# Last level of a graph layer's edge sums as two half levels, with bucket counts kept in SBUF

## The chip, the cores and the metric

One core of a Trainium2 chip runs the kernel. The metric is the device time of one execution in microseconds; a kernel's figure is the median over its runs. The engines are named as the profile names them: PE (TensorE matmul, with PEld for its weight loads), DVE (VectorE), ACT (ScalarE), POOL (GpSimd) and SP (SyncE, which here only issues DMAs).

## What is computed

A graph layer over 12500 nodes of 64 features and 212500 edges that come sorted by `dst`, in float32:

```python
h = jnp.maximum(_layernorm(x, axis=-1), 0.0)
edge_in = jnp.concatenate([h[row], h[col], dist], axis=1)      # row = src, col = dst
e = jax.nn.silu(edge_in @ eW1 + eb1)                           # 129 -> 128
e = jax.nn.silu(e @ eW2 + eb2)                                 # 128 -> 128
agg = jax.ops.segment_sum(e, row, num_segments=h.shape[0])
node_in = jnp.concatenate([h, agg], axis=1)
out = x + jax.nn.silu(node_in @ nW1 + nb1) @ nW2 + nb2
```

## The kernel before

The nodes are cut into NB = 100 **buckets** of L = 125 (node n lies in bucket n mod 100), four buckets make a **quad** (25 quads). `eW1` is split: `ta` and `tb` hold, per node, the parts of the first product that belong to `src` and to `dst`, so an edge needs `ta[src] + tb[dst] + dist * w + b`.

**Sending.** Edges come in `dst` order, in 208 **blocks** of 1024. For a block, `send` (line 406) picks the `tb` rows by a one-hot matmul on a window of neighbouring nodes (`qp`, L418: eight matmuls, float32), ACT copies the result to SBUF tiles `qs` (L429), adds the place of the source node (L435), and POOL scatters it by eight indirect DMAs (L442, 128 rows each) into `q` in DRAM: one slot per edge, ordered by source bucket and by **rank**, the number of the edge within its bucket. `count` (line 338) finds the ranks of the next block: DVE marks each edge's bucket in `oh` (L348) and sums it into `each` (L356); two matmuls (`before`, L382, and, a block later, `rest`, L341) add it to `full`, a PSUM tile that accumulates over all blocks; DVE multiplies `oh` by `full` into `mine` (L396), reduces it to `rank` (L398) and writes the scatter's addresses `to` (L400, four buffers). `pick` (L378) is the one-hot list that `send` needs. `count` and `send` are generators; `send_all` (line 463) steps them in turn, three **pieces** a block, count first.

**Summing.** A bucket's 2304 ranks are split into 12 **levels** (LEVELS, line 54: tiles of 128 ranks per bucket, the block after which they are full, spare ranks that are zeroed beforehand). Batches are (level, quad); a **step** handles four tiles of 128 edges. `fetch` (line 484) loads a quad's ranks `qt` and its `ta` rows `a` through SP, NQ = 4 batches ahead. Per step: `lr` (L518) and `oneT` (L523) turn node numbers into a one-hot; `pt` (L532, L538) transposes the rows and adds `a` by that one-hot; SiLU on ACT (L542); `p2` (L570, with the bias from L564); SiLU (L574); `seg` (L584) sums edges into nodes with the one-hot `one` (L551), in one PSUM bank; `s_add` (L595) adds the sum to `aggT`. In the last level each quad's `nodes` (line 235) then makes the output: `z` (L242, L245), SiLU `zs` (L247), `o` (L251), `os` (L254), and two DMAs.

**Order.** PE, DVE, ACT and SP run in the order written out by hand. `turn` (line 602) lists a step's parts with the number of steps that each is ahead, and four hooks (None). At hooks the loop (line 880) emits send pieces so that level w's blocks, with a lead of three, are sent when its first fetch is due (`marks`), then two pieces of the feed (layer norm, tables), then one stage of a quad's `nodes`. PSUM has `mm` (four tiles, shared by `lr`, `pt`, `qp`, `z`, `o`), `p2` (two), `full` and `seg` (one each).

If a count breaks a level's limits, a flag sends the whole sum through a slow general path.

Of the kernel before, what the change touches and what calls it, by code (L numbers as in the profile page):

```python
# [49 lines left out]
G = 4  # L50
# [4 lines left out]
LEVELS += [(1, 184, 0), (1, 194, 32), (1, 202, 96), (1, 208, 128)]  # L55
ENDS = [P * sum(n for n, _, _ in LEVELS[: w + 1]) for w in range(len(LEVELS))]
# [15 lines left out]
def tile_gnn(ctx: ExitStack, tc: tile.TileContext, x, src, dst, ew, eW1, eb1, eW2, eb2, nW1, nb1, nW2, nb2, out):  # L72
# [105 lines left out]
    rest = const.tile([P, P], BF16, name="rest")  # L178
    nc.vector.tensor_scalar(rest, ahead_i, 0.5, float(G), op0=OP.is_lt, op1=OP.mult)
# [79 lines left out]
    NQ = 4  # L259
# [5 lines left out]
    with ExitStack() as work:  # L265
        mm = work.enter_context(tc.tile_pool(name="mm", bufs=4, space=PSUM))
        p2p = work.enter_context(tc.tile_pool(name="p2", bufs=2, space=PSUM))
        sgp = work.enter_context(tc.tile_pool(name="sg", bufs=1, space=PSUM))
# [5 lines left out]
        full = sgp.tile([P, NB], F32, name="full")  # L274
        nc.tensor.matmul(full, before, identb[:, :NB], start=True, stop=True)
        nc.vector.memset(full, -1.0)
        mine = cnt.tile([P, TB, NB], F32, name="mine")
        sums = []
# [59 lines left out]
        def count(s):  # L338

            if s > 0:  # L340
                nc.tensor.matmul(full, rest, sums.pop(), start=False, stop=True, skip_group_check=True)  # L341
            if s < nblocks:
# [14 lines left out]
                sums.append(each)  # L357
# [9 lines left out]
            for limit, op in limits:  # L367
                nc.vector.tensor_scalar(u, full, float(G * limit - 1), None, op0=op)
                nc.vector.tensor_reduce(v, u, AX.X, OP.max)
                nc.vector.tensor_tensor(bad[:, 1:2], bad[:, 1:2], v, op=OP.add)  # L370
            if s == nblocks:
                return
            if closed and LEVELS[needed[s - 1]][2]:
                nc.vector.tensor_scalar(full, full, float(G * ENDS[needed[s - 1]] - 1), None, op0=OP.max)
            if not whole:
                nc.vector.tensor_scalar(pick, bc, same, plus, op0=OP.is_equal, op1=OP.add)
            elif g == 0:
                nc.vector.tensor_scalar(lists[p][1], lists[p][0], same, plus, op0=OP.is_equal, op1=OP.add)  # L378
            yield
            if g == 0 or not whole:  # L380
                weights(s)
            nc.tensor.matmul(full, before, each, start=False, stop=True, skip_group_check=True)  # L382
# [12 lines left out]
            yield  # L395
            nc.vector.tensor_tensor(mine, oh, full[:, None, :].to_broadcast([P, TB, NB]), op=OP.mult)  # L396
# [66 lines left out]
        def send_all(s0, s1):  # L463

            for s in range(s0, s1):
# [5 lines left out]
                for j, _ in enumerate(itertools.zip_longest(count(s + 1), send(s))):  # L471
                    pending[needed[s]] -= j == PIECES - 1
                    yield


        batches = [(w, B, n) for w, (n, _, _) in enumerate(LEVELS) for B in range(NB // G)]
        steps = [(w, B, n, g) for w, B, n in batches for g in range(n)]
# [4 lines left out]
        most = max(n for _, _, n in batches)  # L482

        def fetch(i):
            if i >= len(batches):
                return
            c, B, n = batches[i]
            assert not any(pending[: c + 1])
            while B not in done_a:
                next(feed)  # L490
            at = B * G * ROWS + G * (ENDS[c] - n * P)
            qt = ld2.tile([P, G * most, W], F32, name="qt")
            ins = nc.sync.dma_start(
                qt[:, : G * n, :].rearrange("p j w -> p (j w)"),
                q[at : at + G * n * P, :].rearrange("(p j) w -> p (j w)", p=P),
            ).ins
# [4 lines left out]
            a = ld2.tile([P, G, H], F32, name="a")  # L501
            nc.sync.dma_start(a, ta_buckets[:, B * G : B * G + G])
            batch[c, B] = [qt, a, None]
            if c == len(LEVELS) - 1:
                node_in[B] = nodes_in(B, ndp[0])

        def of(k):

            c, B, n, g = steps[k]
            return batch[c, B], [((g * G + t) % n * G + (g * G + t) // n, (g * G + t) // n) for t in range(G)]  # L510
# [10 lines left out]
        def s_one_t(k):  # L521
            oneT = wk.tile([L, G, P], F32, name="oneT")
            nc.vector.tensor_scalar(oneT, st[k].pop("lr")[:L], part1[:L, :], None, op0=OP.is_equal)  # L523
            st[k]["oneT"] = oneT

        def s_pt(k):
# [8 lines left out]
            for b, same in itertools.groupby(range(G), lambda t: tiles[t][1]):  # L535
# [6 lines left out]
            nc.scalar.activation(e1, pt, AF.Silu)  # L542
            st[k]["e1"] = e1

        def s_one(k):
            (qt, _, _), tiles = of(k)
            c, B, n, g = steps[k]
            wide = [P, G // n, n, L]
            loc = qt[:, : G * n, H : H + 1].rearrange("p (j b) w -> p b j w", b=G)
            one = wk.tile([P, G, L], F32, name="one")  # L550
# [6 lines left out]
            st[k]["one"] = one  # L557
            if g == n - 1:
                fetch(c * (NB // G) + B + NQ)

# [6 lines left out]
        def s_p2(k):  # L567
            e1, p2 = st[k].pop("e1"), st[k].pop("p2")
            for t in range(G):
                nc.tensor.matmul(  # L570
                    p2[:, t, :], e1[:, t, :], w2, start=False, stop=t == G - 1, skip_group_check=True
                )
            e2 = wk.tile([P, G, H], F32, name="e2")
            nc.scalar.activation(e2, p2, AF.Silu)  # L574
            st[k]["e2"] = e2

        def s_seg(k):
            c, B, n, g = steps[k]
            item, tiles = of(k)
            if g == 0:  # L580
                item[2] = sgp.tile([P, G, L], F32, name="seg")
            e2, one = st[k].pop("e2"), st[k].pop("one")
            for t, (j, b) in enumerate(tiles):
                nc.tensor.matmul(item[2][:, b, :], e2[:, t, :], one[:, t, :], start=j < G, stop=j >= G * (n - 1))  # L584

        def s_add(k):
# [3 lines left out]
            v = aggT[:, B * G : B * G + G, :]  # L590
            seg = batch.pop((c, B))[2]
            if c == 0:
                nc.vector.tensor_copy(v, seg)
            else:
                nc.vector.tensor_tensor(v, v, seg, op=OP.add)  # L595
# [451 lines left out]
```

## Time and profile before

| what | us |
|---|---|
| median of 17 runs (lowest, highest) | 2537.84 (2529.55, 2549.91) |
| the profiled execution, its span | 2538.74, 2537.0 |
| busy: PE, PEld, DVE | 2156.4, 1973.3, 1963.8 |
| busy: ACT, POOL | 1107.1, 1760.9 |
| L442 scatters on POOL, 1661, mean 1043 ns | 1731.7 |
| PE idle before `full` L382, for `each` L356 | 178.6 |
| PE idle before `seg` L584, for `aggT` L595 | 41.6 |
| first and last start of a scatter | 48.4, 2358.5 |

The mean granted clock of PE is 0.939. "Busy" is the time in which an engine executes; a gap has a releaser, what the engine waited for last. "Issue" means that the profile shows no such wait. Matmuls are pipelined, so their mean durations overlap, and the distance from start to start tells what one costs. Each float32 matmul of the program is two instructions of the trace. The kernel's stages by the trace: steps begin at about 278 us; level 7's begin at about 1870 us, and the last level's at 2376 us.

### The profile page before, as it was taken

Reading aid. Unit: us, or ns where it says so; the run is one execution under the profiler, and the core shown is the slowest. Engines: PE = TensorE matmul, PEld = TensorE weight load, DVE = VectorE, ACT = ScalarE, POOL = GpSimd, SP = SyncE. Lnnn points to the kernel's source line nnn. Section 1 sums busy time; section 2 is a strip of 40 time slices with the busy share of each in tenths; the row PEclk is TensorE's granted clock in tenths of the full one; section 3 lists DMA queues with packets and bytes.
Section 4 is the critical chain, followed back from the end, with each engine's and each line's share of the span. In section 5 each row is a group of like instructions: output and inputs, shape, how many; then the busy total and the mean of one; then the engine's idle time right before and its main releaser. Section 6 shows DMA issues by size and latency. Waiting matters only on the chain.

```text
span 2537.0 us, 45519 instructions
## 1 busy us (share of the span) xinstructions
PE 2156.4 (85%) x16193; PEld 1973.3 (78%) x16193; DVE 1963.8 (77%) x2997; ACT 1107.1 (44%) x2408; POOL 1760.9 (69%) x1712
## 2 busy tenths in 40 slices
PE   2664777665698899899999988999999999999997
PEld 1453676555688788888888888888999998999986
DVE  6885787666687788888888888888888888886432
ACT  2442333322344444444444444544555554444442
POOL 3777777777777777777777777777777777752110
PEclk9676888888899999999999999999999999999999
DMA  4563555655666665677555544555555556665652
GB/s 105 175 216 123 185 184 183 195 178 173 191 217 220 219 204 175 220 223 224 193 168 170 168 164 160 168 167 168 180 177 173 180 171 196 198 196 174 191 165 65
DMA packets 229453, 456.96 MB, mean 180 GB/s; under 512 B 43543, under 2 KB 87588, under 8 KB 229013
## 3 DMA queue, kind: packets, MB, share of 16 engines
q1 hardware_dynamic: 151033, 282.94, 34.9%
q0 software_dynamic: 53536, 123.03, 14.1%
q10 hardware_dynamic: 24650, 48.00, 6.5%
q8 instruction: 131, 2.15, 0.4%
q14 instruction: 103, 0.84, 0.1%
HBM read 264.26 MB, written 189.54 MB: 179 GB/s over the span
## 4 chain that ended last, share of the span: by engine, by line
PE 36%; DMA 17%; POOL 16%; DVE 14%; issue 8%; ACT 1%; DVEq 0%; POOLq 0%; SPq 0%; ACTq 0%
POOL q L442 16%; DMA q<-qs,to 14%; PE seg L584 7%; PE pt L538 7%; PE qp L418 7%; PE p L570 6%; PE pt L532 4%; DVE each L356 3%; DVE oneT L523 2%; DVE oh L348 2%; PE lr L518 2%; DVE one L551 2%; DMA qt<-q 1%; DVE aggT L595 1%; DVE mine L396 1%
## 5 line engine op out<-in xcount | busy, mean ns | idle before, releaser
L442 POOL DMA_INDIRECT q<-qs,to x1661 | 1731.7, 1043 | 610.8 <-issue 422.0
L542 ACT ACTIVATE e<-pt 128x512 f32<-128x512 f32 x450 | 268.8, 597 | 735.4 <-PE pt L538 693.6
L418 PEld LDWEIGHTS qp<-win,pick 128*128 128x128 f32 x1664 | 342.6, 217 | 292.1 <-issue 200.0
L584 PE MATMUL seg<-one,e 128*128 128x125 f32 x3600 | 488.4, 279 | 62.1 <-DVE aggT L595 41.6
L584 PEld LDWEIGHTS seg<-one,e 128*128 128x128 f32 x3600 | 447.6, 194 | 73.0 <-issue 33.4
L429 ACT COPY qs<-qp 128x512 f32<-128x512 f32 x418 | 243.2, 584 | 574.3 <-PE qp L418 505.4
L570 PEld LDWEIGHTS p<-w,e 128*128 128x128 f32 x3600 | 467.8, 194 | 26.6 <-issue 7.4
L570 PE MATMUL p<-w,e 128*128 128x128 f32 x3600 | 486.8, 279 | 0.0
L418 PE MATMUL qp<-win,pick 128*128 128x256 f32 x1664 | 476.6, 437 | 11.4 <-DMA win<-tb 7.5
L538 PE MATMUL pt<-oneT,a 125*128 125x128 f32 (+1 forms) x2400 | 471.6, 329 | 3.6 <-DVE oneT L523 3.6
L523 DVE TENSOR_SCALAR oneT<-lr,part 125x512 f32<-125x512 f32 x450 | 335.4, 745 | 88.5 <-PE lr L518 87.8
L538 PEld LDWEIGHTS pt<-oneT,a 125*128 125x128 f32 x2400 | 353.7, 193 | 20.7 <-DVE oneT L523 4.3
L356 DVE TENSOR_REDUCE each<-oh 128x100 bf16<-128x800 bf16 x208 | 315.8, 1518 | 7.2
L551 DVE TENSOR_TENSOR one<-nodes,qt 128x500 f32<-128x500 f32 x450 | 302.2, 672 | 0.0
L532 PE MATMUL pt<-ident,qt 128*128 128x128 f32 x1800 | 278.5, 278 | 0.8 <-DVE oneT L523 0.8
L574 ACT ACTIVATE e<-p 128x512 f32<-128x512 f32 x450 | 268.8, 597 | 4.0 <-PE p L570 3.9
L564 ACT COPY p<-b2f 128x512 f32<-128x512 f32 x450 | 266.6, 593 | 0.0
L595 DVE TENSOR_TENSOR aggT<-aggT,seg 128x500 f32<-128x500 f32 x275 | 184.2, 670 | 87.3 <-PE seg L584 84.5
L400 DVE SCALAR_TENSOR_TENSOR to<-rank,offE 128x8 int32<-128x8 f32 x208 | 36.3, 175 | 244.1 <-DMA q<-qs,to 238.6
L382 PE MATMUL full<-each,before 128*128 128x100 bf16 x208 | 44.4, 214 | 208.8 <-DVE each L356 178.6
L398 DVE TENSOR_REDUCE rank<-mine 128x8 f32<-128x800 f32 x208 | 205.1, 986 | 7.2
L396 DVE TENSOR_TENSOR mine<-oh,full 128x800 f32<-128x800 bf16 x208 | 203.9, 980 | 2.5 <-PE full L382 2.5
(134 smaller groups left out, 1597.2 us busy)
## 6 DMA issues: line engine op xcount, KB each, us to landing
qt<-q SPq DMA_DIRECT2D x150, 576.0 KB
a<-ta SPq DMA_DIRECT2D x300, 256.0 KB
qt<-q SPq DMA_DIRECT2D x150, 288.0 KB
q<-zeros ACTq DMA_DIRECT2D x25, 1080.0 KB
q<-qs,to POOLq DMA_INDIRECT x1661
bc<-dests SPq DMA_DIRECT2D x103, 256.0 KB
q<-zeros ACTq DMA_DIRECT2D x10, 1440.0 KB
win<-tb SPq DMA_DIRECT2D x208, 58.0 KB
```

Of the source, the lines that this page charges most:

```text
L356: nc.vector.tensor_reduce(each, oh.rearrange("p t b -> p b t"), AX.X, OP.add)
L418: nc.tensor.matmul(qps[t // 2][:, t % 2, :k], pick[:, t * P : (t + 1) * P], win[:, :k], start=True, stop=True)
L442: ins = nc.gpsimd.indirect_dma_start(out=q[:], out_offset=bass.IndirectOffsetOnAxis(ap=to[:k, j : j + 1], axis=0), in_=qs[:k, t % 2, a, :] ...
L523: nc.vector.tensor_scalar(oneT, st[k].pop("lr")[:L], part1[:L, :], None, op0=OP.is_equal)
L532: nc.tensor.matmul(pt[:, t, :], qt[:, j, :H], ident, is_transpose=True, start=t == 0, stop=False, skip_group_check=True)
L538: nc.tensor.matmul(pt[:, cols, :], a[:L, b, :], oneT[:, cols, :], start=False, stop=True, skip_group_check=True)
L542: nc.scalar.activation(e1, pt, AF.Silu)
L551: nc.vector.tensor_tensor(one.rearrange("p (b j) l -> p b j l", j=n), nodes1[:, None, None, :].to_broadcast(wide), loc[:, tiles[0][1] : ti ...
L564: nc.scalar.copy(p2, b2f)
L570: nc.tensor.matmul(p2[:, t, :], e1[:, t, :], w2, start=False, stop=t == G - 1, skip_group_check=True)
L574: nc.scalar.activation(e2, p2, AF.Silu)
L584: nc.tensor.matmul(item[2][:, b, :], e2[:, t, :], one[:, t, :], start=j < G, stop=j >= G * (n - 1))
```

## The change

- The last level (one tile of 128 ranks, full after block 208) becomes two of half a tile: 64 ranks full after block 205, 64 after 208. A step of a half level takes two quads: a tile holds 64 ranks of one bucket and 64 of another, so four tiles cover eight buckets. Its `pt` has eight matmuls of 64 columns for `a`, its `seg` eight matmuls on 64 rows each, into two banks, and `s_add` adds both. 25 quads make 13 such steps a half level, 26 in all.
- `full` moves from PSUM to SBUF, with a running `base`. Two matmuls of a block, now together, write `here` (a tile of `mm`), and two DVE adds follow: `full` is `base` plus what precedes, `base` grows by the block's sum. Limits are read from `base`.
- `seg` gets the bank that `full` had: two banks.
- `pick` and the load of weights come before the limits; in each piece `send` comes before `count`.
- `fetch` loads a quad's half level by two DMAs and both quads' `a` by one; three batches ahead for half levels. Two stages of `nodes` are emitted at a hook.

```diff
-LEVELS += [(1, 184, 0), (1, 194, 32), (1, 202, 96), (1, 208, 128)]
+LEVELS += [(1, 184, 0), (1, 194, 32), (1, 202, 96), (0.5, 205, 64), (0.5, 208, 64)]
...
-    rest = const.tile([P, P], BF16, name="rest")
-    nc.vector.tensor_scalar(rest, ahead_i, 0.5, float(G), op0=OP.is_lt, op1=OP.mult)
+    every = const.tile([P, P], BF16, name="every")
+    nc.vector.memset(every, float(G))
...
-        sgp = work.enter_context(tc.tile_pool(name="sg", bufs=1, space=PSUM))
+        sgp = work.enter_context(tc.tile_pool(name="sg", bufs=2, space=PSUM))
...
-        full = sgp.tile([P, NB], F32, name="full")
-        nc.tensor.matmul(full, before, identb[:, :NB], start=True, stop=True)
-        nc.vector.memset(full, -1.0)
+        base = cnt.tile([P, NB], F32, name="base")
+        nc.vector.memset(base, -1.0)
+        full = cnt.tile([P, NB], F32, name="full")
...
         def count(s):
-            if s > 0:
-                nc.tensor.matmul(full, rest, sums.pop(), start=False, stop=True, skip_group_check=True)
...
-                sums.append(each)
+                if not whole:
+                    nc.vector.tensor_scalar(pick, bc, same, plus, op0=OP.is_equal, op1=OP.add)
+                elif g == 0:
+                    nc.vector.tensor_scalar(lists[p][1], lists[p][0], same, plus, op0=OP.is_equal, op1=OP.add)
+            yield
+            if s < nblocks and (g == 0 or not whole):
+                weights(s)
...
-            nc.tensor.matmul(full, before, each, start=False, stop=True, skip_group_check=True)
+            here = mm.tile([P, 2, NB], F32, name="here", tag="mm")
+            nc.tensor.matmul(here[:, 0], before, each, start=True, stop=True)
+            nc.tensor.matmul(here[:, 1], every, each, start=True, stop=True)
...
+            nc.vector.tensor_tensor(full, base, here[:, 0], op=OP.add)
+            nc.vector.tensor_tensor(base, base, here[:, 1], op=OP.add)
             nc.vector.tensor_tensor(mine, oh, full[:, None, :].to_broadcast([P, TB, NB]), op=OP.mult)
...
-                for j, _ in enumerate(itertools.zip_longest(count(s + 1), send(s))):
+                for j, _ in enumerate(itertools.zip_longest(send(s), count(s + 1))):
...
+                if n < 1:
+                    for h in range(2):
+                        part_ = q[at : at + rows, :].rearrange("(r h j) w -> r h (j w)", h=2, j=2)[:, h, :]
+                        to = qt[h * HB : (h + 1) * HB, 2 * (b - B) : 2 * (b - B) + 2, :]
+                        load_ready(c, nc.sync.dma_start(to.rearrange("p j w -> p (j w)"), part_).ins)
...
+            a = (ld2 if m == 1 else ld3[0]).tile([P, m * G, H], F32, name=f"a{m}")
+            nc.sync.dma_start(a, ta_buckets[:, B * G : (B + m) * G])
...
+        def fetch_to(i):
+            while fetched[0] < len(batches) and fetched[0] <= i + (NQ if batches[fetched[0]][3] == 1 else NH):
+                fetch(fetched[0])
+                fetched[0] += 1
...
+            for t, h in itertools.product(range(nt), range(2)) if steps[k][2] < 1 else ():
+                cols = slice(h * HB, (h + 1) * HB)
+                b = t // 2 * G + 2 * h + t % 2
+                nc.tensor.matmul(
+                    pt[:, t, cols], a[:L, b, :], oneT[:, t, cols], start=False, stop=True, skip_group_check=True
+                )
...
+                item[2] = [sgp.tile([P, G, L], F32, name="seg") for _ in range(2 if n < 1 else 1)]
...
+            for t, h in itertools.product(range(len(tiles)), range(2)) if n < 1 else ():
+                rows = slice(h * HB, (h + 1) * HB)
+                nc.tensor.matmul(
+                    item[2][h][:, t, :], e2[rows, t, :], one[rows, t, :], start=True, stop=True
+                )
...
-                    if tails and next(tails[0], 0) == 0:
-                        tails.pop(0)
+                    for _ in range(min(2, len(tails))):
+                        if tails and next(tails[0], 0) == 0:
+                            tails.pop(0)
```

## The prediction

> **What bounds the kernel now.** I read the chain of waits first, then what POOL waited for, then busy time by stretch, then single instructions.
>
> ```profile
> PE 36%; DMA 17%; POOL 16%; DVE 14%; issue 8%; ACT 1%; DVEq 0%; POOLq 0%; SPq 0%; ACTq 0%
> ```
>
> No engine owns the chain; it hops between PE, the scatters (POOL and their DMA) and DVE. So I asked what POOL, the engine that issues the scatters of L442, waits for between 60 and 1870 us (columns: total us, times, longest).
>
> ```profile
> POOL q L442 <- issue: 346.1, 1135, 0.3
> ...
> POOL q L442 <- ACT qs L435: 3.7, 12, 0.3
> ```
>
> Every wait is the same 0.3 us gap between two scatters; the 12 waits on ACT are that gap too. For 1800 us POOL never lacks work: it is saturated, and its "77% busy" is all it can show with a gap behind each scatter. A block has eight scatters: 8 x (1043 + 300 ns) = 10.7 us a block. Waits of PE and DVE in this stretch are back-pressure and are worth nothing. By stretch (PE, PEld, DVE, ACT, POOL busy; clock; DMA share; GB/s):
>
> ```profile
> 200.00:1653.00 1453.00, 1204.32 (x8640) 1097.90 (x8639) 1143.70 (x1720) 607.58 (x1314) 1121.35 (x1085) 0.93 0.58 188
> 1653.00:1870.00 217.00, 208.21 (x1600) 195.33 (x1599) 186.42 (x280) 109.02 (x231) 168.32 (x160) 0.99 0.52 171
> 1870.00:2076.00 206.00, 202.99 (x1596) 191.86 (x1595) 180.12 (x270) 107.25 (x226) 159.25 (x153) 1.00 0.52 172
> 2076.00:2287.00 211.00, 201.43 (x1762) 195.72 (x1762) 181.22 (x278) 103.24 (x214) 146.33 (x139) 0.99 0.62 196
> 2287.00:2376.00 89.00, 88.15 (x824) 87.36 (x823) 56.24 (x91) 43.56 (x91) 23.48 (x24) 1.00 0.59 185
> 2376.00:2537.00 161.00, 145.57 (x1167) 126.98 (x1165) 57.40 (x100) 59.14 (x122) 15.97 (x22) 0.96 0.42 129
> ```
>
> PE is 83%, then 96%, then 95 to 99% busy. Cut at 1870 us (start of level 7's steps): **before it POOL sets the pace, behind it PE does**, and the last 161 us are the 25 steps of the last level with the node products between them.
>
> **The change, part by part.** It is summed against the profiled run, 2538.7 us (span 2537.0), 0.9 above the median 2537.84.
>
> *Counts in SBUF.* Matmuls per block stay two. What moves is where DVE's `mine` (L396) reads `full`: from PSUM to SBUF. Compare two scatters with the DVE instruction that runs beside each (start, duration):
>
> ```profile
> 1604.61 0.97 POOL L442 DMA_INDIRECT q<-qs,to  x1 [0.30 <-issue]
> ...
> 1609.69 1.18 POOL L442 DMA_INDIRECT q<-qs,to  x1 [0.30 <-issue]
> ```
>
> ```profile
> 1604.53 0.98 DVE L396 TENSOR_TENSOR mine<-oh,full 128x800 f32<-128x800 bf16 x1
> ...
> 1609.06 0.98 DVE L348 TENSOR_TENSOR oh<-nodes,bkE 128x800 bf16<-128x800 f32 x1
> ```
>
> Beside `mine` the scatter takes its usual 0.97. Beside `oh` it takes 1.18 and ends 0.83 after `oh` ends: it stood still from about 0.13 us in until `oh` was done. I counted this over all scatters: of those with `oh` running 0.127 us after their start 125 of 145 were over 0.997 us; with `one` (L551) 111 of 152; with `mine` 5 of 147; with `oneT` (L523, input in PSUM) 1 of 225; with `aggT` (L595, one input in PSUM) 2 of 85. So what stalls a scatter is an elementwise DVE instruction with two inputs in SBUF, and `mine` escapes only because `full` is in PSUM. In SBUF it becomes like `oh`: scatters that end 0.84 us behind an `oh` carry 54.2 us of excess, 54.2 / 208 = 0.26 us a block. Up to 1870 us POOL has no slack, and 172 - 3 = 169 `mine` run there: 169 x 0.26 = **+44 us**. Bounds: 0, if it stays like today's `mine`; 147 x 125/145 x 464 ns (mean excess beside `oh`) = 59 us over 208 blocks, or 55 over the 196 up to 2186 us where POOL is still fed. I take the row of `oh`: same size, 980 against 985 ns.
>
> The Trainium skill bears on this (SBUF — State Buffer, section Who interferes with whom): a DVE instruction with two SBUF inputs contends with a GpSimd one that reads SBUF, as the counts above show, but the page also tells of a probe in which tensor_tensor did not stall a DMA issued from GpSimd, and infers that descriptors need only the write side. By that probe `mine` would cost nothing and the time would be near 2564; by the row it is near 2608. The trace's stalls beside `oh` are of just this kind, so the row decides.
>
> The two adds on DVE (`full`, `base`, 128x100, one input in PSUM, so no stall): L368 of that size takes 254 ns, L391 with 128 columns 292; about 0.27 each, 0.53 us a block. Up to 1870 they hide under POOL's pace (DVE is 79 to 86% busy, 0.53 of 10.7 is 5%). Behind it they hide under PE: `oneT` and `each`, which PE waits for, have a step's lead. All 36 blocks uncovered would be 19 us; I take +3, since PE's waits on DVE there are small (below); bounds 0 and 19. An extra PSUM tile per block in the pool of four can hold `pt` back until `oneT` has read `lr`; that is within the same bound.
>
> *Picks ahead, sends ahead of counts, second bank for sums.* They remove PE waits. Behind 1870 us only these are left:
>
> ```profile
> PE seg L584 <- DVE aggT L595: 3.7, 3, 1.4
> ...
> PE full L382 <- DVE each L356: 0.8, 2, 0.5
> ```
>
> So -3 us, bounds -5 and 0. The page's 178.6 us (`each`) and the rest of 41.6 us (`aggT`) lie before 1870, where POOL paces; worth 0, and between 700 and 1870 us 29.9 + 37.9 = 68 us if POOL had slack. Picks move on DVE only past count limits; the weight load (one issue on SP) stays in its piece.
>
> *The last level as two halves.* The send schedule does not move: the goal at level 11's first fetch was all 600 pieces and still is (3 x 197 + 9 = 600), at the same step. The steps go from 25 to 26, 24 of four tiles and two of two. What differs on PE, from the last level's rhythm:
>
> ```profile
> 2406.28 0.69 PE L245 MATMUL z<-hrn,w1n 64*128 64x250 f32 x4
> 2406.90 1.16 PE L570 MATMUL p<-w,e 128*128 128x128 f32 x8
> 2407.90 0.98 PE L251 MATMUL o<-w2n,zs 128*125 128x64 f32 x8
> 2408.72 1.11 PE L584 MATMUL seg<-one,e 128*128 128x125 f32 x8
> ...
> 2410.34 1.06 PE L538 MATMUL pt<-oneT,a 125*128 125x128 f32 x8
> 2411.23 1.01 PE L242 MATMUL z<-aggT,w1g 128*128 128x250 f32 x4
> ```
>
> From start to start, eight 128-column matmuls take 0.89 us (2410.34 to 2411.23) and eight 64-column ones 0.82 (2407.90 to 2408.72): half the columns save 8%, as each needs its own weights. The half step has 16 of 64 columns for `pt` in place of 8 of 128: 1.64 against 0.89, +0.75. A plain step is 3.345 us (the sum lr 0.23, transposes 0.44, and three times 0.89), so 24 x 4.095 + 2 x 2.05 (half of everything) = 102.4 against 25 x 3.345 = 83.6: **+19 us**. Bounds 0 (cost by columns) and +21 (as many as full ones). `seg` becomes 16 matmuls on 64 rows, the halves alternating. Four matmuls on 64 rows take 0.62 (2406.28 to 2406.90) where four on 128 take 0.94 (L242, to L245's next start): 0.66, so pairs overlap; 2 x 0.66 x 0.89 = 1.17, +0.28 a step or +7. Perfect overlap 0, none +22; I take **+5**, as alternation favours pairs. PE does the same node products (5.89 us a step with them, less 3.345, times 25: 64 us), now two quads a step; at the end two more quads than now drain with bare waits for ACT and DVE, +2 (0 to 6). DVE does 2.8 us of 4.1 in a half step: hidden. `a` is read once more (6.4 MB) and a quad's rows come in two loads: 807 KB per 4.1 us is 197 GB/s, where the trace reaches 220; SP issues five loads a step (2 us). Taken as 0, bound +10, as PE would wait for `qt`.
>
> **Sum.** 2538.7 + 44 + 3 - 3 + 19 + 5 + 2 = 2608.7, less 0.9: **2608 us**.
>
> **Rivals.** *Mine does not stall* (18%): if reading the narrow `oh` leaves the second port free, the 44 drops out and the rest stays: 2564, range 2550 to 2580. Against it: `oh` and `one` stall alike whatever their types. *PE's waits were the pace* (9%, the faster side): if `each` and `aggT` really hold the kernel between 700 and 1870 us, up to 68 us go and the tail's 26 stay: 2538.7 - 68 + 26 = 2497. It decides for faster once more than 26 us are won. For it: PE is in 36% of the chain. Against it: POOL's waits above. *DVE becomes the bound* (5%): 208 x 0.53 = 110 on top of the tail, and above the 44 where both hold: 2638 to 2675. It needs DVE idle under 0.53 a block; it has (206.0 - 180.1) / 19 = 1.4 in level 7. *The fallback runs* (2%): the flag is raised and the general sums cost many milliseconds. With the reference's edges every bucket has at least 2197 places filled where 2176 are asked at block 205, and at most 2285 of 2304 at the end, so hardly.
>
> **How the numbers follow.** The forecast has 66%, by itself 2585 to 2635 (`mine` 0.19 to 0.28 a block, the tail 12 to 40). The 80% range adds the first rival: 2553 to 2635. A measurement here tells 0.2% (5 us) from no change; faster by more takes the second rival, 0.09; within it 0.03 from the rivals' edges; slower 0.88.
>
> **What would show it.** Right: the scatters' mean rises from 1043 to about 1075 ns, those beside `mine` end 0.84 behind it; level 7's steps begin about 44 us later; the last two levels' steps run at 4.1 us without nodes; POOL's gaps stay 0.3. Wrong: scatters beside `mine` still 0.97; gaps of POOL on ACT before 1870 (then PE or DVE paces); 64-column matmuls at half price; PE waiting for `qt` in half steps.

## The result, and the profile after

| | median, us | lowest, highest | runs |
|---|---|---|---|
| before | 2537.61 | 2529.55, 2549.91 | 46 |
| after | 2614.73 | 2609.48, 2627.18 | 8 |

The ratio is 1.0309, with a 95% interval of [1.0295, 1.0324]: the change costs 77 us. The forecast was 2608. The profiled execution of the kernel after took 2623.07 us, 8 more than the median, so its stages add to a little more than 77.

The chain of waits of the kernel after has nearly the make-up that it had:

```profile
PE 30%; DMA 19%; POOL 17%; DVE 16%; issue 9%; ACT 2%; DVEq 0%; SPq 0%; POOLq 0%; ACTq 0%
```

So, as before, the reading starts with POOL: the group of the scatters on the page (busy, mean ns of one, idle before), and what POOL waited for from 60 us to the start of level 7's steps, now at 1912 us.

```profile
L442 POOL DMA_INDIRECT q<-qs,to x1661 | 1778.5, 1071 | 610.6 <-issue 418.4
```

```profile
POOL q L442 <- issue: 340.3, 1114, 0.9
```

The gaps stayed 0.3 us; the scatters themselves grew from 1043 to 1071 ns. POOL is still saturated up to level 7, and level 7 begins 42 us later. Here is a usual scatter and one beside `mine` (start, duration), first POOL's rows, then DVE's:

```profile
1607.03 0.97 POOL L442 DMA_INDIRECT q<-qs,to  x1 [0.30 <-issue]
1608.30 1.64 POOL L442 DMA_INDIRECT q<-qs,to  x1 [0.30 <-issue]
```

```profile
1607.66 0.25 DVE L394 TENSOR_TENSOR full<-base,here 128x100 f32<-128x100 f32 x1
1607.94 0.26 DVE L395 TENSOR_TENSOR base<-base,here 128x100 f32<-128x100 f32 x1
1608.12 0.98 DVE L396 TENSOR_TENSOR mine<-oh,full 128x800 f32<-128x800 bf16 x1
```

`mine` runs until 1609.10, the scatter until 1609.94: 0.84 us behind it, like those beside `oh`. Of the scatters that had `mine` running 0.127 us after their start, 103 of 140 took more than 0.997 us; in the kernel before it was 5 of 147. The excess of those over the usual 967 ns sums to 37.8 us. The same rows show what the two adds cost DVE: 0.25 and 0.26 us.

That `mine` sets the start of level 7 shows in a sum over POOL's records: ahead of level 7 there are 1348 scatters before and 1349 after, their durations make 1404.9 and 1446.5 us, +41.6, and the gaps between them 416.6 and 417.8.

The prediction takes two inputs in SBUF for what stalls a scatter. They are not all of it: `pick` (a TENSOR_SCALAR that reads one tile, `bc`, and two scalars a partition) stalls one too, and later in its course:

```profile
1624.72 1.24 POOL L442 DMA_INDIRECT q<-qs,to  x1 [0.31 <-issue]
```

```profile
1625.04 0.80 DVE L357 TENSOR_SCALAR pick<-bc,same,plus 128x1024 f32<-128x1024 bf16 x1
```

`pick` begins 0.32 us into the scatter, and the scatter ends 0.12 us behind it. Of the scatters into which a `pick` came 0.1 to 0.4 us after their start, all were longer than 0.997 us: 53 of 53 in the kernel before, 71 of 71 in the kernel after. An instruction with two inputs in SBUF (`oh`, `one`, or `eq` of `count`) that begins after the scatter leaves it alone: 4 of 363 such scatters were longer in the kernel before. The scatters that met a `pick` carry some 19 us of excess in both kernels, so this is no part of the 77.

By stretch (busy PE, PEld, DVE, ACT, POOL; clock; DMA share; GB/s), cut at the starts of levels 6, 7, 8, 10 and 11 and at the start of the second half level:

```profile
1690.00:1912.00 222.00, 210.22 (x1616) 196.53 (x1616) 196.60 (x323) 110.70 (x233) 173.05 (x161) 0.98 0.51 171
1912.00:2119.00 207.00, 203.78 (x1600) 190.98 (x1599) 188.65 (x309) 107.81 (x226) 161.09 (x151) 1.00 0.51 171
2119.00:2330.00 211.00, 196.46 (x1725) 190.09 (x1724) 184.94 (x305) 101.14 (x210) 150.83 (x141) 0.99 0.62 194
2330.00:2425.00 95.00, 93.33 (x871) 92.38 (x871) 60.09 (x101) 45.25 (x94) 21.62 (x21) 1.00 0.58 180
2425.00:2482.50 57.50, 57.50 (x601) 54.58 (x599) 31.50 (x51) 20.44 (x40) 1.48 (x2) 1.00 0.60 178
2482.50:2621.00 138.50, 120.40 (x951) 100.88 (x949) 40.27 (x78) 40.11 (x86) 17.16 (x24) 0.92 0.43 123
```

The profiled span is 2621.3 us, 84.3 longer than that of the kernel before. From these starts: +42 up to level 7 (1912 against 1870), +7 from there to the last ranks (513 against 506), and +35.5 in the tail (196.2 against 160.7). One execution gives such a start to some 10 us only: `e8` and `e9` below have the same program up to level 7, and there it began at 1901 and 1902 us in theirs. PE is 93 to 100% busy in the stretches from 1912 to 2482.5, so there every us of PE's work counts. Its steps in the half levels:

```profile
2425.78 0.39 PE L543 MATMUL lr<-identb,qt 128*125 128x128 bf16 x4
2426.01 0.61 PE L558 MATMUL pt<-ident,qt 128*128 128x128 f32 x4
2426.45 1.90 PE L565 MATMUL pt<-oneT,a 125*128 125x64 f32 x16
2428.19 1.11 PE L614 MATMUL p<-w,e 128*128 128x128 f32 x8
2429.23 1.16 PE L629 MATMUL seg<-one,e 64*128 64x125 f32 x16
2430.32 0.44 PE L543 MATMUL lr<-identb,qt 128*125 128x128 bf16 x4
```

From start to start, `pt`'s 16 matmuls of 64 columns take 1.74 us, `p` 1.04 and `seg` 1.09, where each group of eight had 0.89. A half step takes 4.585 us on average, a plain one took 3.345. Then, where the node products begin, PE waits for `qt` three times within 7 us, and its matmuls take twice their time:

```profile
2484.04 0.30 PE L543 MATMUL lr<-identb,qt 128*125 128x128 bf16 x2 [0.51 <-DMA qt<-q]
2489.62 0.30 PE L543 MATMUL lr<-identb,qt 128*125 128x128 bf16 x2 [1.07 <-DMA qt<-q]
2490.89 0.30 PE L543 MATMUL lr<-identb,qt 128*125 128x128 bf16 x2 [0.97 <-DMA qt<-q]
...
2494.30 1.98 PE L242 MATMUL z<-aggT,w1g 128*128 128x250 f32 x4
```

```profile
2475.00:2491.00 16.00, 13.45 (x137) 12.48 (x137) 8.10 (x14) 4.60 (x9) 3.38 (x4) 1.00 0.74 216
2491.00:2507.00 16.00, 15.26 (x75) 12.08 (x75) 3.30 (x6) 3.17 (x7) 2.89 (x4) 0.57 0.51 151
```

The four `z` took 1.01 us in the kernel before, here 1.98; the mean granted clock of the window (third figure from the right) is 0.57 in place of 1.00. It was 0.50 for 13.7 us, from 2492.0 to 2505.6:

```profile
2488.60:2492.00 3.40, 1.41 (x14) 1.33 (x14) 2.02 (x4) 0.00 (x0) 0.72 (x1) 1.00 0.68 184
2492.00:2505.60 13.60, 13.04 (x57) 10.34 (x55) 2.25 (x4) 2.51 (x5) 2.89 (x4) 0.50 0.53 155
```

In the 3.4 us ahead of the fall PE was busy for 1.41. The records of the granted clock change only at multiples of 3.413 us from the first one, between 1.00 and 0.50. Cut on that grid, each stretch at the full clock in which PE was busy for less than 40% was followed by one at half the clock: 31 of 31 in the kernel before, 37 of 37 in the kernel after. With PE busy for 65% or more it was 0 of 559 and 1 of 566; between, 14 of 48 and 6 of 56.

### The profile page after: what moved, and what is told of

The parts are those of the page before. It is cut to its first block, busy times and chain, and to the rows that moved or that the text cites. A ratio compares the mean times of both kernels' runs of the same rounds, so it can differ in the third digit from the quotient of the medians.

```text
span 2621.3 us, 46834 instructions
## 1 busy us (share of the span) xinstructions
PE 2187.3 (83%) x16592; PEld 1997.8 (76%) x16592; DVE 2065.7 (79%) x3449; ACT 1113.0 (42%) x2411; POOL 1808.1 (69%) x1712
## 3 DMA queue, kind: packets, MB, share of 16 engines
q0 software_dynamic: 53536, 123.03, 13.7%
## 4 chain that ended last, share of the span: by engine, by line
PE 30%; DMA 19%; POOL 17%; DVE 16%; issue 9%; ACT 2%; DVEq 0%; SPq 0%; POOLq 0%; ACTq 0%
POOL q L442 17%; DMA q<-qs,to 17%; PE p L614 6%; PE pt L571 6%; PE seg L635 5%; PE qp L418 3%; PE pt L558 3%; DVE oneT L549 3%; DVE oh L345 2%; DVE each L353 2%; DMA qt<-q 2%; DVE one L595 2%; PE lr L543 2%; PE pt L565 2%; DVE aggT L651 1%
## 5 line engine op out<-in xcount | busy, mean ns | idle before, releaser
L442 POOL DMA_INDIRECT q<-qs,to x1661 | 1778.5, 1071 | 610.6 <-issue 418.4
L571 PE MATMUL pt<-oneT,a 125*128 125x256 f32 (+1 forms) x2200 | 462.8, 344 | 57.4 <-DVE oneT L549 57.2
L418 PE MATMUL qp<-win,pick 128*128 128x256 f32 x1664 | 435.0, 408 | 58.7 <-DMA pick<-in_edge_weight_dram 39.2
L635 PE MATMUL seg<-one,e 128*128 128x125 f32 x3400 | 461.0, 279 | 5.1 <-DVE one L595 4.0
L635 PEld LDWEIGHTS seg<-one,e 128*128 128x128 f32 x3400 | 423.8, 196 | 6.5 <-ACT e L618 4.8
L418 PEld LDWEIGHTS qp<-win,pick 128*128 128x128 f32 x1664 | 325.6, 205 | 108.6 <-issue 42.3
L595 DVE TENSOR_TENSOR one<-nodes,qt 128x500 f32<-128x500 f32 x425 | 286.2, 673 | 0.0
L651 DVE TENSOR_TENSOR aggT<-aggT,seg 128x500 f32<-128x500 f32 (+1 forms) x302 | 198.9, 666 | 86.7 <-PE seg L635 54.0
L543 PE MATMUL lr<-identb,qt 128*125 128x128 bf16 x1800 | 182.8, 225 | 48.4 <-DMA qt<-q 40.3
L558 PEld LDWEIGHTS pt<-ident,qt 128*128 128x128 f32 x1800 | 195.8, 145 | 22.1 <-DVE oneT L549 19.2
```

Of the source, the lines that this page charges most:

```text
L418: nc.tensor.matmul(qps[t // 2][:, t % 2, :k], pick[:, t * P : (t + 1) * P], win[:, :k], start=True, stop=True)
L442: ins = nc.gpsimd.indirect_dma_start(out=q[:], out_offset=bass.IndirectOffsetOnAxis(ap=to[:k, j : j + 1], axis=0), in_=qs[:k, t % 2, a, :] ...
L558: nc.tensor.matmul(pt[:, t, :], qt[:, j, :H], ident, is_transpose=True, start=t == 0, stop=False, skip_group_check=True)
L571: nc.tensor.matmul(pt[:, cols, :], a[:L, b, :], oneT[:, cols, :], start=False, stop=True, skip_group_check=True)
L595: nc.vector.tensor_tensor(one.rearrange("p (b j) l -> p b j l", j=n), nodes1[:, None, None, :].to_broadcast(wide), loc[:, tiles[0][1] : ti ...
L635: nc.tensor.matmul(item[2][0][:, b, :], e2[:, t, :], one[:, t, :], start=j < G, stop=j >= G * (n - 1))
```

## The experiments

The theory: three parts, `mine` reading SBUF (it stalls the scatters), the half levels (more matmuls) and the rest (adds, extra PSUM tile, order). The main rival: the stalls are real but cover nothing, and the half levels or the rest make the loss. Each part was undone from the kernel after, and done alone in the kernel before.

The first four runs and the last came on a chip where the kernel before itself took 3133 and 3078 us, and the granted clock was about 0.87 in place of 0.94, so each counts only beside the kernel before on that chip. (In `e4` 93 stretches of the clock's grid had PE busy for less than 40%, and in the same kernel on a usual chip, `e11`, 36: the lower clock goes with a PE that waits more.)

**First four runs.** In `e1_mine_from_psum` the add writes into PSUM and `mine` reads it there; the rest is the kernel after:

```diff
-            nc.vector.tensor_tensor(full, base, here[:, 0], op=OP.add)
+            nc.vector.tensor_tensor(here[:, 0], base, here[:, 0], op=OP.add)
...
-            nc.vector.tensor_tensor(mine, oh, full[:, None, :].to_broadcast([P, TB, NB]), op=OP.mult)
+            nc.vector.tensor_tensor(mine, oh, here[:, 0][:, None, :].to_broadcast([P, TB, NB]), op=OP.mult)
```

> The changed kernel, with one thing undone: base + here is written back into here (PSUM), and mine reads its second input there, not from SBUF. The two DVE adds, the matmuls and the half levels stay. Port theory (a scatter stands still beside a DVE instruction with two SBUF inputs): the stalls beside mine vanish, level 7's steps begin some 42 us earlier than in the changed kernel, total 2570 to 2578. Rival, the two adds a block load DVE too much: nothing changes, 2610 to 2620. Rival, the order of send and count or the extra PSUM tile costs the time: 2610 to 2620 too.

`e2_before_mine_from_sbuf` does the opposite to the kernel before:

```diff
+            held = wk.tile([P, NB], F32, name="held")
+            nc.vector.tensor_copy(held, full)
-            nc.vector.tensor_tensor(mine, oh, full[:, None, :].to_broadcast([P, TB, NB]), op=OP.mult)
+            nc.vector.tensor_tensor(mine, oh, held[:, None, :].to_broadcast([P, TB, NB]), op=OP.mult)
```

> The kernel before, with one thing done: full is copied from PSUM to SBUF by DVE (128x100, some 0.25 us a block) and mine reads the copy. Nothing else of the change. Port theory: about 100 of 140 scatters that meet mine stand still, level 7's steps begin some 42 us later than before, total 2578 to 2588. Rival, DVE load: one small copy a block, half of the change's adds, gives at most 10 to 20 us, with no stalls beside mine. Rival, order of send and count: no change, 2538.

`e3_whole_last_level` is the kernel after with one whole last level:

```diff
-LEVELS += [(1, 184, 0), (1, 194, 32), (1, 202, 96), (0.5, 205, 64), (0.5, 208, 64)]
+LEVELS += [(1, 184, 0), (1, 194, 32), (1, 202, 96), (1, 208, 128)]
```

> The changed kernel with the last level whole again (one tile of 128 ranks, full after block 208), so batches of one quad to the end; counts in SBUF, second bank and order stay. If the half steps are the tail's cost, all of the last two levels' 35 us comes back: 2576 to 2582, and level 7 still begins near 1912. If most of the tail's cost were the sends or the second bank, less than 10 us come back.

`e4_whole_level_and_psum` has the edits of `e1` and `e3`.

> Both undone at once: mine from PSUM and a whole last level; what is left of the change is the order (send ahead of count, picks ahead), here with its two adds, and the second bank for sums. If the two costs are separate they add: 2614 - 43 - 35 = 2536, and the bank's gain of 3 us behind level 7 would make it 2530 to 2538. If the adds or the order have a price of their own: 2545 to 2560.

| run | median, us | ratio to before [95%] | scatters stalled beside `mine` |
|---|---|---|---|
| `e1` | 3179.74 | 1.0171 [1.0115, 1.0227] | 1 of 152 |
| `e2` | 3084.02 | 0.9869 [0.9812, 0.9925] | 72 of 84 |
| `e3` | 3108.67 | 0.9958 [0.9913, 1.0003] | 117 of 147 |
| `e4` | 3160.04 | 1.0072 [1.0037, 1.0106] | 1 of 160 |

The stalls come and go with the place of `full`, as the theory says, but here they carry no price: `mine` from SBUF was even the faster way. POOL's waits in `e4` from 60 to 2600 us say why no price is to be had (total us, times, longest):

```profile
POOL q L442 <- ACT qs L435: 557.6, 151, 9.8
POOL q L442 <- issue: 394.3, 1283, 1.4
```

On this chip POOL waits for `qs` for 558 us; the scatters are not the pace, and a longer scatter only shortens such a wait. Why SBUF is faster here is argued, not shown: a `full` or `here` that `mine` no longer reads is free sooner, and PE waits less for PSUM. PE's waits, first of `e3`, then of `e4`:

```profile
PE pt L558 <- ACT qs L429: 103.1, 52, 5.2
```

```profile
PE pt L558 <- ACT qs L429: 151.8, 69, 9.8
```

All four missed the times expected of them. They could not decide the theory, since they did not have the bound that it speaks of. So the deciding ones were repeated on chips where the kernel before takes its usual 2538 to 2542 us.

**Mine, undone and alone.** `e5_mine_from_psum_again` is `e1` again, `e10_before_mine_from_sbuf_again` is `e2`.

> The same kernel as e1, on another chip: the one of the first four runs had its kernel before at 3133 us, a granted clock of 0.87 and POOL waiting for ACT, so that scatters were not the pace there. Where the kernel before takes about 2537 us, the port theory wants 2570 to 2578 (ratio 1.013 to 1.016), level 7 at some 1870 us, and under 5 of 140 scatters beside mine stalled. DVE's load or the order of send and count as the cause: 2610 to 2620 (1.03).

Measured: 2582.37 us, 1.0154 [1.0137, 1.0172]. The scatters' mean is back at 1043 ns, 1 of 151 beside `mine` is stalled, and level 7 begins at 1873 us.

> The same kernel as e2, for a chip where the kernel before takes about 2537 us and POOL is saturated up to level 7. Port theory: 70 to 75 in 100 scatters that meet mine stand still, 2572 to 2588 (ratio 1.014 to 1.019). If DVE's load or PE's waits held the pace: 2538 to 2550.

Measured: 2592.51 us, 1.0191 [1.0162, 1.0220]. That is 4 us above the range expected. Beside `mine` 75 of 91 scatters are stalled, with 43.6 us of excess, and level 7 begins at 1919 us. Its group of scatters (the edit moves the line by two):

```profile
L444 POOL DMA_INDIRECT q<-qs,to x1661 | 1788.9, 1077 | 610.3 <-issue 418.6
```

So the stall costs 1.55% where it is taken from the kernel after (1.0309 less 1.0154, 39 us of 2538) and 1.9% where it is put into the kernel before (48 us, with a copy of `full` in it; the medians of those runs differ by 54). It lies before level 7: `e5` wins all of it there, 1873 against 1912, and `e10` loses 49 there and 8 more between level 7 and the last ranks. The durations of the scatters ahead of level 7 sum to 1408.1 us in `e5` and 1452.8 in `e10`, 3 and 48 more than in the kernel before. As `e5` keeps both adds, DVE's load does not make the stall's price.

**The rest alone.** `e11_whole_level_and_psum_again` is `e4` again: what remains of the change is two adds, the extra tile `here`, the order, the second bank and two stages of `nodes` at a hook.

> The same kernel as e4, for a chip like the one of e5. The order, the two adds and the second bank for sums alone: mine's stall took 39 us (1.0309 to 1.0154) and the tail's rest is 1.0154, so 2530 to 2541 (ratio 0.997 to 1.000). Above 1.004 the order or the adds have a price of their own; below 0.994 the second bank is worth more than the 3 us behind level 7.

Measured: 2548.78 us, 1.0043 [1.0029, 1.0057], 11 us, where 2530 to 2541 was expected: not zero. Level 7 begins at 1876 us (+6), the last ranks at 2386 (+10), and the tail takes 162.8 (+2). PE's waits on the whole run, then those behind 1876 us:

```profile
PE pt L571 <- DVE oneT L549: 46.6, 33, 3.9
```

```profile
PE lr L543 <- DMA qt<-q: 16.7, 11, 2.4
```

In the kernel before the first was 3.6 us and the second, behind 1870, 7.8. The first lies almost wholly ahead of level 7, where POOL paces; the second is about 9 us more on PE's own path, of which the stages behind level 7 show 6. Of the 6 us ahead of level 7, 4 are longer scatters (their durations there sum to 1408.9 us against 1404.9), not beside `mine`; what lengthened them was not shown. As `e5` and `e11` differ in the last level alone, the half levels cost 1.0154 - 1.0043 = 1.1%, 28 us, the dip of the clock included (`e5` has it too: 0.50 for 13.7 us from 2450.0).

`e12_order_alone` was to split the 11 us. It is the kernel before with the order of the change: counts in PSUM, one bank, a whole last level.

```diff
+                if not whole:
+                    nc.vector.tensor_scalar(pick, bc, same, plus, op0=OP.is_equal, op1=OP.add)
+                elif g == 0:
+                    nc.vector.tensor_scalar(lists[p][1], lists[p][0], same, plus, op0=OP.is_equal, op1=OP.add)
+            yield
+            if s < nblocks and (g == 0 or not whole):
+                weights(s)
             limits = [(SURE[w], OP.is_gt) for w in ready_at if s == ready_at[w]]
...
-                for j, _ in enumerate(itertools.zip_longest(count(s + 1), send(s))):
+                for j, _ in enumerate(itertools.zip_longest(send(s), count(s + 1))):
```

> The kernel before with only the order of the change: picks and weight loads ahead of the count limits, and send ahead of count in each piece. Counts stay in PSUM, one bank for sums, a whole last level. It splits the 11 us (1.0043 [1.0029, 1.0057]) that remained with counts in SBUF, mine reading PSUM and a whole last level. Theory A, the two DVE adds and the extra tile of the pool make them: ratio 0.998 to 1.001, level 7 at about 1870 us as in the kernel before, PE's wait of lr for qt behind 1870 us about 8 us, of pt for oneT before 1870 us about 4 us. Theory B, the order makes them: ratio about 1.004, level 7 about 6 us later, the wait of lr for qt about 16 us. Both in part: between.

Measured: 3058.86 us, 0.9975 [0.9940, 1.0010], beside a kernel before of 3078.0 us, on the chip of the first four runs. There the order alone loses nothing, while `e4`, the order with adds, tile and second bank, lost 0.7%; the intervals do not meet. That speaks for the adds, the tile or the bank. But POOL was not the pace in this run (its waits for `qs` make 471.9 us), so neither the start of level 7 nor the wait for `qt` could be compared. On the usual chip the split stays open.

**The half levels' dip.** SP issues a half step's loads together with those of the nodes. The profile times them (SP's queue, start and time of a group):

```profile
2479.85 2.37 SPq L503 DMA_DIRECT2D qt<-q  x4
2482.32 0.53 SPq L508 DMA_DIRECT2D a<-ta  x1
2482.89 0.87 SPq L118 DMA_DIRECT2D xr<-in_x_dram  x2
2483.82 0.34 SPq L232 DMA_DIRECT2D hrn<-hd  x1
2484.21 0.87 SPq L118 DMA_DIRECT2D xr<-in_x_dram  x2
2485.12 0.34 SPq L232 DMA_DIRECT2D hrn<-hd  x1
2485.88 3.25 SPq L503 DMA_DIRECT2D qt<-q  x4
```

One step's issues take 6.0 us (2479.85 to 2485.88) where a half step takes 4.6: SP falls behind, `qt` comes late. `e9_node_loads_one_step_later` starts the node loads a step later; `e8_node_loads_from_act` has ACT issue them.

```diff
-            while fetched[1] < min(fetched[0], i + NH - 1):
+            while fetched[1] < min(fetched[0], i + NH - 2):
```

> The changed kernel with the node loads begun one batch later (for the batch whose one is being made, not the next), so that SP issues them for two fast half steps before node products slow the steps, not for three. In e8 the loads left SP's queue, lr still waited 0.85 us for qt, and ACT then held zs up by 3.7 us, so the clock fell all the same. If SP's backlog before the first nodes is the cause of the dip in the changed kernel: qt is late by under 1.5 us, no stretch with the clock under 0.9, the last level some 9 us shorter (138.6 to 130), total near 2606. If the node products then wait for their loads, the dip comes back: 2612 to 2620.

Measured: 2606.28 us, 1.0254 [1.0234, 1.0274]. The waits for `qt` are gone, and the clock of the same window is whole:

```profile
2491.00:2507.00 16.00, 15.26 (x126) 12.98 (x125) 5.12 (x9) 5.74 (x12) 2.39 (x4) 1.00 0.55 161
```

PE does 126 matmuls there where it did 75. The tail takes 187.7 us in place of 196.2: the dip cost 8.5. (The ratio fell by 0.55%, 14 us; the 5 beyond the tail lie ahead of the last ranks, where no effect of this edit is shown, and the two intervals leave room for them.)

```diff
-        rows16(nc.sync.dma_start, xr, x_rows[:, b : b + G, :])
+        rows16(nc.scalar.dma_start, xr, x_rows[:, b : b + G, :])
...
-        nc.sync.dma_start(hr, hd[:, b // 2 : b // 2 + G // 2, :])
+        nc.scalar.dma_start(hr, hd[:, b // 2 : b // 2 + G // 2, :])
```

> The changed kernel, but x rows and hd rows for the node products are loaded from ACT's queue, not SP's. In the changed kernel SP's issues for one half step with node loads took 5.7 us where a step takes 4.6; lr waited 2.5 us for qt near 2490 us and the granted clock fell to 0.57 for 16 us. If SP's issue time is the cause: no wait of lr there, clock 1.00 in the last level, some 10 us less from level 11's first step to the end (196 to 186), total 2600 to 2608 where the changed kernel has 2615. If the loads' bytes are the cause: no change.

Measured: 2638.22 us, 1.0377 [1.0342, 1.0412], worse than the kernel after. `lr` waited only 0.8 us for `qt`, but the loads now stand in ACT's queue ahead of `zs`, and PE waits for `zs` (waits from 2430 us on):

```profile
PE o L251 <- ACT zs L247: 18.1, 15, 3.7
ACT zs L247 <- DMA xr<-in_x_dram: 15.1, 6, 4.2
```

In the kernel after PE's wait for `zs` was 3.9 us; the tail grew to 212.8. In this run the load took its wait for a free buffer along to the other queue.

**The stall turned round.** If `mine` escapes in the kernel before because one input is in PSUM, `oh` and `one`, which stall scatters in both kernels, should escape as well when the node numbers are there. `e6_before_node_numbers_in_psum` is the kernel before with that constant beside `full`, in one PSUM tile:

```diff
-        full = sgp.tile([P, NB], F32, name="full")
+        held = sgp.tile([P, NB + L], F32, name="full")
+        full, nodesP = held[:, :NB], held[:, NB:]
...
+        nc.vector.tensor_copy(nodesP, nodes1)
...
-                    nodes1[:, None, :NB].to_broadcast([P, TB, NB]),
+                    nodesP[:, None, :NB].to_broadcast([P, TB, NB]),
...
-                nodes1[:, None, None, :].to_broadcast(wide),
+                nodesP[:, None, None, :].to_broadcast(wide),
```

> The kernel before, with the constant row of node numbers that oh and one compare with copied once into the bank of full, so that both have one input in PSUM. Port theory: their stalls go (93 us of POOL's 119 us of stalls), the scatters' mean falls from 1043 to about 985 ns, a block from 10.7 to 10.3 us, and level 7 begins 40 to 70 us earlier: 2470 to 2500 (ratio 0.973 to 0.985). If PE or DVE holds the pace up to level 7 anyway: the mean falls but the time stays above 2525.

Measured: 2655.68 us, 1.0448 [1.0431, 1.0466]: a miss in the time, not in the stalls. None of 165 scatters beside `oh` and 3 of 201 beside `one` are stalled, and the scatters' mean is 983 ns. But the waits from 700 to 1900 us show what the shared tile brings:

```profile
POOL q L444 <- ACT qs L437: 139.3, 90, 4.3
...
PE full L384 <- DVE one L553: 95.4, 55, 2.8
DVE oh L350 <- PE full L343: 63.4, 92, 2.0
```

PE's write of `full` waits for DVE's read of the constant in the same tile, and DVE for PE's write; POOL then lacks `qs`. `e7_node_numbers_own_bank` gives the constant a tile and a PSUM bank of its own, in the kernel of `e4` (a whole level, `mine` from PSUM, one bank for `seg`):

```diff
-        sgp = work.enter_context(tc.tile_pool(name="sg", bufs=2, space=PSUM))
+        sgp = work.enter_context(tc.tile_pool(name="sg", bufs=1, space=PSUM))
...
+        nodesP = sgp.tile([P, L], F32, name="nodesP")
+        nc.vector.tensor_copy(nodesP, nodes1)
```

> The changed kernel with mine from PSUM and a whole last level (as e4), one bank for sums again, and the node numbers for oh and one in the freed bank as a tile of their own, written once. In e6 the same copy shared a tile with full, and 95 us of PE's waits were full for one, 63 us of DVE's oh for full: waits of the shared tile. Port theory: the scatters' mean is near 985 ns as in e6, POOL's gaps stay 0.3 for longer, level 7 begins 40 to 70 us before 1870, total 2470 to 2500 (ratio 0.973 to 0.985): faster than both kernels. If reading the constant from PSUM has itself a price, or PE and DVE cannot follow: 2520 to 2560.

Measured: 2486.14 us, **0.9774 [0.9742, 0.9806]**, faster than both kernels. The group of scatters, and one of them with the `oh` beside it:

```profile
L444 POOL DMA_INDIRECT q<-qs,to x1661 | 1638.0, 986 | 651.0 <-issue 409.5
```

```profile
1506.40 0.97 POOL L444 DMA_INDIRECT q<-qs,to  x1 [0.30 <-issue]
1507.67 0.97 POOL L444 DMA_INDIRECT q<-qs,to  x1 [0.30 <-issue]
```

```profile
1506.87 0.98 DVE L347 TENSOR_TENSOR oh<-nodesP,bkE 128x800 bf16<-128x800 f32 x1
```

`oh` runs from 1506.87 to 1507.85; the scatter that starts at 1507.67 takes its 0.97 all the same. Level 7 begins at 1813 us, 57 earlier than in the kernel before. The kernel that `e7` starts from is that of `e11` (1.0043), so the move is worth 2.7%, some 68 us. Of the 32 us of excess that its scatters keep, 19 are beside `pick`.

## Why the prediction was right, point by point

- **POOL paces up to level 7, PE behind it.** Right. The gaps kept at 0.3 us (one wait of 3.6 us for ACT's `var` aside, which the prediction passed over), and what lengthened the scatters came out in the start of level 7: 1870, 1912, 1919 and 1813 us at scatter means of 1043, 1071, 1077 and 986 ns (before, after, `e10`, `e7`).
- **`mine` in SBUF, +44.** Right in mechanism and size: 39 us undone (`e5`), 48 done alone (`e10`), 42 in the start of level 7. The row decided against the probe in the Trainium skill (SBUF — State Buffer, section Who interferes with whom): the indirect scatters do stall beside a tensor_tensor, 103 of 140 with both inputs in SBUF, 1 of 151 with one in PSUM. The page's rule of two SBUF inputs agrees with that. Its inference that such an instruction leaves descriptors alone is not refuted: a scatter also takes its addresses `to` from SBUF, and a tensor_tensor that began after the scatter left it alone. But "two inputs in SBUF" is too narrow for a rule of these scatters: `pick` stalls them as well.
- **Adds and extra tile +3, waits removed -3.** Mis-sized. The sum of the two terms was 0, and `e11` gives 11 us. The bounds of the adds (0 to 19) held it. The prediction looked for PE's wait on `oneT` and `each`; what showed on PE's path is 9 us more wait for `qt` behind level 7. `one`, which releases `qt`'s buffer, is later when DVE has 0.51 us more a block; that link is argued. It explains at most the 6 us behind level 7; the rest lies ahead of it. `pt` held back by the pool's extra tile came as said, 46.6 us, and lies mostly under POOL's pace.
- **Half steps, +24 on PE.** Mechanism right, a little small. A half step is 1.24 us longer, where 1.03 was predicted: `pt` +0.85 (0.75), `seg` +0.20 (0.28), `p` +0.15 (0), `lr` +0.04 (0). 24 x 4.585 + 2 x 2.3 less 83.6 makes +31. Half the columns indeed save almost nothing. Against it stands a gain that the prediction did not have: a half step with the nodes of two quads takes 9.27 us (`lr` at 2524.80, 2534.07 and 2543.34), so a quad's nodes cost 2.34 in it where they cost 2.545 before, 5 us less over the level.
- **DMA and SP at 0, bound +10.** The value taken was wrong, the bound held: 8.5 us. The working counted five loads and 2 us a step (SP's rows show 2.9 us, `qt` x4 and `a`), and left out the six that the nodes of two quads add, so that SP's issue exceeds the step; and the price is mostly the clock, not the 2.5 us of waits themselves. With the drain (+2), the tail was 26 in the sum; it measured 35.5 in the profile, the dip included (31 + 8.5 - 5 leave 1 for the drain), 27 without the dip; as a ratio of whole runs (`e5` to `e11`), the dip included, 28 with some 6 us of uncertainty.
- **The sum.** Measured 39 + 28 + 11 = 78, predicted 44 + 26 + 0 = 70. That the three make up the whole is no test: each is a difference of neighbouring ratios, from 1.0309 down to 1. The tests are `e10`, which puts the stall alone into the kernel before, and the stages. That the total is off by only 7 us is partly luck: 5 too much for `mine` stands against 11 too little for the adds and 2 for the tail, and in the tail too little for the half steps and the dip against too much for the nodes.
- **The rivals.** *Mine does not stall* fell with 103 of 140. *PE's waits were the pace* fell: in the kernel after those for `aggT` are gone and those for `each` went from 178.6 to 146.6 us, while POOL's gaps stayed 0.3 us and level 7 began no earlier; the wait of `pt` for `oneT` grew from 3.6 to 57.2 us and that of `lr` for `qt` from 17.4 to 40.3. *DVE becomes the bound* fell: from 1912 to 2482.5 PE is 93% busy and more, DVE at most 91%. The fallback did not run.

Open are the split of the 11 us on the usual chip, and why the chip of the first four runs and the last is slower at the same program. The chains of those five runs put 7 to 11% of the span down to another core or an unknown queue, those of the other runs none; what that was, the traces do not say.

## What to carry to other kernels

Where GpSimd's indirect DMAs set the pace, ask of every DVE instruction beside them how many inputs it has in SBUF, and count the long scatters beside each, as one input did not save `pick`. Here a small constant operand in PSUM, in a tile that nobody writes, freed the scatters of `oh` and `one`, and a value that PE already left in PSUM should be read there. Cutting a step's tiles in half halves neither its matmuls' time nor its DMA issues: count both per step, the issues of neighbouring work on the same queue included. A cost is only as dear as the bound it sits on, so look for that bound in each run before comparing.

## What was not expected of the hardware

- Waits that were each 1.07 us or shorter, some 2 us of the 2.5 ahead of 2491 us, were followed by half the clock for 13.7 us. The Trainium skill (TensorE: Matmul & The Clock Gate, section Part 1: The HAM clock gate) puts the fall behind about 3.4 us of idle. `e8` agrees, with one gap of 3.66 us up to 2495.44 and half the clock from 2495.1; the kernel after had no gap that long in this place. By the counts on the 3.413 us grid, a stretch need not be idle: less than 40% busy was enough each time.
- A scatter was held up in two ways: at its start by an instruction with two SBUF inputs that was already running, and then it ended 0.84 us behind that; or by a `pick` that began 0.1 to 0.4 us into it, and then it ended 0.12 us behind the `pick` (71 of 71 in the kernel after). An instruction with two SBUF inputs that began inside the scatter left it alone (5 of 466 longer there).
- One tile shared by a constant and an accumulator made PE and DVE wait for each other, 95.4 and 63.4 us in 1200 us (`e6`), where a tile and bank of its own made none of it (`e7`). These are waits on the program's semaphores; whether two tiles in one bank would have done was not run.
- The same program took 3078 to 3133 us on one chip, at a granted clock of about 0.87, with POOL no longer the pace; there `mine` from SBUF, 1.9% slower on the usual chip, was 1.3% faster (0.9869 [0.9812, 0.9925]).
